# Moving three small steps of a Householder tridiagonalisation between VectorE and GpSimd, and dropping a negated scalar

## The chip, the cores and the metric

The kernel runs on one core of a Trainium2 chip. The metric is the device time of one execution in microseconds, as the median of several runs. Engines are called by their names in the profile: PE (TensorE, matrix products), PEld (TensorE loading weights), DVE (VectorE), ACT (ScalarE), POOL (GpSimd) and SP (SyncE, which issues the DMAs here).

## The reference

Two graph layers run one after the other over 64 items x of 256 x 256 (float32), with one shared 256 x 256 matrix `adj`. Cut to what matters:

```python
h = relu(layernorm(x))
# layer 0: G = adj * adj, three products with weights, G applied in each
y = relu(G @ (h @ W1)); y = relu(G @ (y @ W2)); x = x + G @ (y @ W3)

h = relu(layernorm(x))
# layer 1: eigenvectors of the normalized Laplacian of adj
deg = adj.sum(0) + adj.sum(1) - diag(adj); d = rsqrt(deg)
U = eigh(d[:, None] * (diag(deg) - adj) * d[None, :]).vectors
x = x + U @ (relu(U.T @ h @ L1_W1 + b1) @ L1_W2 + b2)
```

Layer 0 needs nothing of the eigenvectors. Layer 1 needs them, and layer 0's result.

## The kernel before, in words

**Two works side by side.** The eigenvectors U of a 256 x 256 symmetric matrix are found by one long chain of dependent steps: a reduction to tridiagonal form (`tridiagonalize`, lines 410 to 553), the eigenproblems of 16 small leaves (`leaves`), and a merge in four levels (`level`). That chain uses mostly VectorE with small operands. Meanwhile TensorE works off layer 0 for 32 pairs of items (`Layers.products`, with matmuls of 128x512 and 128x256), and ScalarE empties its PSUM banks. When the eigenvectors are there, layer 1 runs over the same 32 pairs (`layer1`).

**Who decides the order.** On TensorE and ScalarE the order is written down when the program is built, by `Pace` (lines 147 to 230). Pace keeps a clock for each engine and reckons how long each operation of the eigenvector chain takes, from its engine and width (`Op`, lines 83 to 117: for VectorE 0.065 us plus 0.06 for a scalar from memory plus an amount by width, for GpSimd 0.2 us plus an amount by width, all times 1.06 for the chain). Each time the chain wants an operation, Pace first issues layer-0 operations that start before the chain's operation is due. On the chip TensorE then runs that list strictly in order: if the chain is later than Pace reckoned, TensorE stands at the chain's transposes; if it is earlier, the chain waits for the layer-0 products ahead of it. Layer-0 work that finds no place beside the chain is issued beside the first pairs of layer 1 (`pace.finish()` in line 2070 issues what is left). On VectorE and GpSimd the order is chosen by a scheduler of the tile framework. All issued operations of the chain carry line 192 in the profile, so they are told apart by their tiles.

**One column of the reduction.** The loop in line 470 runs over 254 columns. Column `k` with `lo = k + 1` below 128 works on both halves of the 256 rows (`halves = [0, 1]`, 127 columns, called the wide half here); from 128 on only the second half is left (the narrow half). The matrix `a` lies in SBUF as two halves of 128 partitions x 256. `xr` holds the current column as a row on all partitions, `xc` the same as a column. In each column:

- `rs` and `qs` and from them `nb` (line 484) give the sign and length of the reflection. `nb` and `alpha` are columns of the tile `m1`, the sums of squares (`tail`) of `m2`; all three show as `m` in the profile.
- `xa` (line 482) is the product of the two halves of `a` with `xr`, one wide operation for each half, tile `r` in the profile; `ac` (line 487) adds the own column.
- TensorE turns `ac` and the matrix's own column into rows, `pu` (psB) and `pr` (psA), with transposes against the identity (line 488).
- Beside that, `u1` (line 496) is the first element of the reflection vector, written into `xr`; `den` (line 497) the divisor, `none` a guard against a zero column; `gam` (line 498) its reciprocal (tile `z`, column k); `uc` (line 499, tile `q`) the vector as a column; `ngam` (line 500) is `gam` with its sign turned; `gg` and `gu` are products with it.
- `gc` and `gr` (lines 504 and 508) are the products scaled with `ngam`; `uau` is their scalar product; `both`, `f` and `xn` (lines 511 to 513) make the next column as a row, `xcn` (lines 525 to 527) the same as a column, with a mask from `lower` in line 527.
- Four wide operations (lines 532 and 533, two for each half) update `a`, tile `A`.
- `below` and `length` (lines 443 to 462) start the next column's length: `alpha` on GpSimd, the sum of squares on ScalarE in the wide half, `q` and `qn` on the engine `aside(lo)`, which is GpSimd in the wide half and VectorE in the narrow half. `none` is on GpSimd in both.

GpSimd's queue in a column of the wide half is, in this order: `alpha` (a copy into m), `q`, `none`, `qn`, `none`, `qs`, `gg`, `gu`. It issues no DMA; all DMAs are issued by SP.

```python
aside = lambda lo: nc.gpsimd if lo < P else nc.vector
```

Of the kernel before, what the change touches and what calls it, by code (L numbers as in the profile page):

```python
# [23 lines left out]
OP = mybir.AluOpType  # L24
# [4 lines left out]
P = 128  # L29
# [222 lines left out]
class Eigen:  # L252
# [44 lines left out]
    def row(self, tag):  # L297
        return self.mp.tile([P, N], F32, tag=tag, name=tag)
# [111 lines left out]
    def tridiagonalize(self, a):  # L410

        nc = self.nc
        ident = self.ident
        us, gams = self.mat("q2"), self.row("z2")
        drow, erow = self.row("D"), self.row("E")  # L420
        nc.vector.memset(erow[:, N - 1 : N], 0.0)
        nc.vector.memset(us[:, :, N - 2 : N], 0.0)
        nc.vector.memset(gams[:, N - 2 : N], 0.0)

        def as_row(tag, column, halves):
            ps = self.psum(tag)
            for h in halves:
                nc.tensor.transpose(
                    ps[:, h * P : (h + 1) * P],
                    column[:, h : h + 1].to_broadcast([P, P]),  # L430
                    ident[:, 0, 0:P],
                )
            return ps

        row = lambda tag: self.sp.tile([P, N], F32, tag=tag, name=tag)
        guard = self.col("guard", 1)
        nc.vector.memset(guard, 1e-30)
        book = self.mat("m1")
        alphas, nbs, tails = book[:, 0, :], book[:, 1, :], self.mat("m2")[:, 0, :]

        aside = lambda lo: nc.gpsimd if lo < P else nc.vector

        def below(xr, lo):

            rest = slice(lo + 1, N)
            sq, tail, alpha = self.row("junk"), *(t[:, lo - 1 : lo] for t in (tails, alphas))
            if lo < P:
                nc.scalar.activation(sq[:, rest], xr[:, rest], AF.Square, accum_out=tail)
            else:
                self.stt(sq[:, rest], xr[:, rest], 1.0, xr[:, rest], OP.mult, OP.mult, accum=tail)  # L450
            nc.gpsimd.tensor_copy(alpha, xr[:, lo : lo + 1])
            return alpha, tail

        def length(xr, lo, tail):

            nn, s0, q, qn = (self.col(c, 1) for c in ("nn", "s0", "q", "qn"))
            x1 = xr[:, lo : lo + 1]
            self.stt(nn, x1, x1, tail, OP.mult, OP.add)
            nc.scalar.activation(s0, nn, AF.Sqrt, bias=guard)
            aside(lo).tensor_scalar(q, x1, 0.0, 0.5, OP.is_ge, OP.subtract)  # L460
            aside(lo).tensor_tensor(qn, q, nn, OP.mult)
            return nn, s0, q, qn

        xc = self.col("xc")
        self.tt(xc, a[:, :, 0], self.lower[:, :, 0], OP.mult)
        xr = row("xr")
        nc.vector.tensor_copy(xr, as_row("psB", xc, [0, 1])[:, 0:N])
        alpha, tail = below(xr, 1)
        nn, s0, q, qn = length(xr, 1, tail)
        for k in range(N - 2):  # L470
            lo = k + 1
            r, rest = slice(lo, N), slice(lo + 1, N)
            halves = [0, 1] if lo < P else [1]
            hs = slice(halves[0], H)
            rc = a[:, :, lo]

            rs, qs, nb = self.col("rs", 1), self.col("qs", 1), nbs[:, k : k + 1]
            self.recip(rs, s0)
            aside(lo).tensor_tensor(qs, q, s0, OP.mult)
            xa, junk = self.col("xa"), self.row("r0")  # L480
            for h in halves:
                self.stt(junk[:, r], a[:, h, r], 1.0, xr[:, r], OP.mult, OP.mult, accum=xa[:, h : h + 1])
                if h == halves[0]:
                    self.stt(nb, rs, qn, qs, OP.mult, OP.add)

            ac, uc = self.col("ac"), us[:, :, k]
            self.stt(ac[:, hs], rc[:, hs], nb, xa[:, hs], OP.mult, OP.add)
            pu, pr = as_row("psB", ac, halves), as_row("psA", rc, halves)

            none = self.col("none", 1)  # L490
            nc.gpsimd.tensor_scalar(none, tail, 1e-30, 1e30, OP.is_le, OP.mult)
            nc.gpsimd.tensor_tensor(none, none, nn, OP.add)
            den, ngam, gg, gu = (self.col(c, 1) for c in ("den", "ngam", "gg", "gu"))
            gam = gams[:, k : k + 1]
            u1 = xr[:, lo : lo + 1]
            self.ts(u1, u1, nb, OP.add)
            self.stt(den, alpha, nb, none, OP.mult, OP.add)
            self.recip(gam, den)
            self.stt(uc, ident[:, :, lo], nb, xc, OP.mult, OP.add)
            self.ts(ngam, gam, -1.0, OP.mult)  # L500
            aside(lo).tensor_tensor(gg, gam, gam, OP.mult)
            aside(lo).tensor_tensor(gu, gg, u1, OP.mult)
            gc, gr = self.col("gc"), row("gr")
            self.ts(gc[:, hs], ac[:, hs], ngam, OP.mult)

            uau, c = self.col("uau", 1), self.col("c", 1)
            self.stt(junk[:, r], pu[:, r], 1.0, xr[:, r], OP.mult, OP.mult, accum=uau)
            self.ts(gr[:, r], pu[:, r], ngam, OP.mult)

            xn, xcn, both, f = row("xr"), self.col("xc"), self.row("r1"), self.col("f", 1)  # L510
            self.stt(both[:, rest], gr[:, rest], u1, pr[:, rest], OP.mult, OP.add)
            self.stt(f, uau, gu, gr[:, lo : lo + 1], OP.mult, OP.add)
            self.stt(xn[:, rest], xr[:, rest], f, both[:, rest], OP.mult, OP.add)
            more = lo + 1 < N - 1
            if more:
                alpha1, tail1 = below(xn, lo + 1)
            self.stt(c, uau, 0.5, gg, OP.mult, OP.mult)
            wr, wc = row("wr"), self.col("wc")
            self.stt(wr[:, r], xr[:, r], c, gr[:, r], OP.mult, OP.add)
            self.stt(wc[:, hs], uc[:, hs], c, gc[:, hs], OP.mult, OP.add)  # L520
            if more and halves[0]:
                following = length(xn, lo + 1, tail1)
            if halves[0]:
                nc.gpsimd.memset(xcn[:, 0:1], 0.0)
            self.stt(xcn[:, hs], gc[:, hs], u1, rc[:, hs], OP.mult, OP.add)
            self.stt(xcn[:, hs], uc[:, hs], f, xcn[:, hs], OP.mult, OP.add)
            self.tt(xcn[:, hs], xcn[:, hs], self.lower[:, hs, lo], OP.mult)
            if more and not halves[0]:
                following = length(xn, lo + 1, tail1)

            for h in halves:
                self.stt(a[:, h, r], wr[:, r], uc[:, h : h + 1], a[:, h, r], OP.mult, OP.add)
                self.stt(a[:, h, r], xr[:, r], wc[:, h : h + 1], a[:, h, r], OP.mult, OP.add)
            xr, xc = xn, xcn
            if more:
                alpha, tail, (nn, s0, q, qn) = alpha1, tail1, following

        done = slice(0, N - 2)
        e0 = self.row("r1")[:, done]
        self.tt(e0, nbs[:, done], alphas[:, done], OP.add)  # L540
        self.ts(tails[:, done], tails[:, done], 1e-30, OP.is_gt)
        self.tt(e0, e0, tails[:, done], OP.mult)
        self.tt(erow[:, done], alphas[:, done], e0, OP.subtract)

        nc.vector.tensor_copy(erow[:, N - 2 : N - 1], xr[:, N - 1 : N])
        dc = self.col("dnew")
        junk = self.row("junk")
        for h in range(H):
            self.stt(junk, a[:, h, :], 1.0, ident[:, h, :], OP.mult, OP.mult, accum=dc[:, h : h + 1])
        pb = self.psum("psB")  # L550
        self.spread(pb[:, 0:N], dc, ident)
        self.ts(drow, pb[:, 0:N], 1.0, OP.add)
        return drow, erow, us, gams
# [1593 lines left out]
```

## Time and profile before

| | |
|---|---|
| median of 3 runs | 2461.46 us (2460.98 to 2461.79) |
| the profiled execution | 2461.43 us, its span in the profile 2459.6 us |
| PE busy over the span | 2397.0 us (97%), 8986 matmuls |
| PEld busy | 1545.5 us (63%) |
| DVE busy | 2147.1 us (87%), 13352 instructions |
| ACT busy | 1008.9 us (41%) |
| POOL busy | 475.5 us (19%), 1625 instructions |
| wide half of the reduction | 21.45 to 781.83 us |
| narrow half | 781.83 to 1332.40 us |
| leaves, levels, eigenvectors | to 2261.6 us |
| layer 1 | to the end |

Busy time is the time in which an engine has an instruction in work. VectorE's instructions overlap: the next one starts before the one ahead has written its last element, so what an instruction costs in a row of others is the distance of the starts. A matrix product of float32 stands as two matmuls in the trace. In lines of the timeline, the columns are start in us, duration in us, engine, line, operation, output<-inputs, shapes, count, and in brackets the idle time before it and what ended it. Buffer numbers are left out of names, so that `m` is any column of the tile m1 or m2, and `A` the matrix.

### The profile page before, as it was taken

How to read it: one execution, taken by the hardware profiler on the slowest of the kernel's cores; microseconds unless marked ns; L12 is line 12 of the kernel's file. 1: busy time of each engine (PE TensorE's matmuls, PEld its weight loads, DVE VectorE, ACT ScalarE, POOL GpSimd, SP SyncE). 2: the span in 40 equal slices, each digit the busy share in tenths (PEclk: the TensorE clock that was granted, in tenths of full speed). 3: DMA queues.
4: the chain of work that ended last, by engine and by line, in shares of the span. 5: the costliest groups of instructions: out<-in, count | busy, mean ns of one | idle time of the engine just before them, and what ended most of it. 6: DMA issues, size and time to landing. Idle time of an engine off the chain costs nothing. (4 is left out here: it accounts for less than half of the span.)

```text
span 2459.6 us, 38181 instructions
## 1 busy us (share of the span) xinstructions
PE 2397.0 (97%) x8986; PEld 1545.5 (63%) x8986; DVE 2147.1 (87%) x13352; ACT 1008.9 (41%) x2827; POOL 475.5 (19%) x1625
## 2 busy tenths in 40 slices
PE   7999999999999999999999999999999999999999
PEld 4666655666555566655556666655566666666888
DVE  7999999999999999999999989888887888885333
ACT  4334444434444433444444244443434344443322
POOL 2333333333333111111111000000000000000443
PEclk9999999999999999999999999999999999999999
DMA  3000000000000000000000000000000000001476
GB/s 112 18 5 23 22 18 23 22 22 6 22 21 20 22 23 14 14 23 22 18 23 30 10 22 22 22 22 18 22 22 27 20 8 22 22 22 36 167 256 202
DMA packets 59401, 90.02 MB, mean 37 GB/s; under 512 B 5793, under 2 KB 42785, under 8 KB 59169
## 3 DMA queue, kind: packets, MB, share of 16 engines
q1 hardware_dynamic: 59168, 87.52, 10.6%
q8 instruction: 73, 1.20, 0.2%
q14 instruction: 160, 1.30, 0.2%
HBM read 47.13 MB, written 40.37 MB: 36 GB/s over the span
## 5 line engine op out<-in xcount | busy, mean ns | idle before, releaser
L192 PE MATMUL bank<-y,L_gnn_W 128*128 128x512 f32 x2048 | 906.5, 593 | 0.3 <-ACT y L192 0.3
L192 PEld LDWEIGHTS bank<-y,L_gnn_W 128*128 128x128 f32 x2048 | 379.3, 190 | 427.6 <-issue 409.4
L192 PE MATMUL bank<-L_gnn_W,s 128*128 128x256 f32 x2048 | 464.6, 379 | 1.7 <-ACT s L192 1.6
L192 PEld LDWEIGHTS bank<-L_gnn_W,s 128*128 128x128 f32 x2048 | 382.1, 190 | 51.4 <-ACT s L192 2.0
L192 ACT ACTIVATE s<-bank 128x512 f32<-128x512 f32 x384 | 224.8, 587 | 188.3 <-PE bank L192 187.1
L192 PE MATMUL bank<-gt,s 128*128 128x256 f32 x1024 | 230.5, 379 | 2.0 <-ACT s L192 2.0
L192 PE MATMUL bank<-L_gnn_W,y 128*128 128x512 f32 x512 | 228.9, 593 | 0.0
L192 PEld LDWEIGHTS bank<-gt,s 128*128 128x128 f32 x1024 | 191.9, 190 | 37.0 <-issue 9.8
L192 ACT ACTIVATE s<-nn,guard 128x1 f32<-128x1 f32 x254 | 74.3, 293 | 244.9 <-DVE nn L192 230.5
L192 ACT ACTIVATE junk<-xr 128x254 f32<-128x254 f32 (+63 forms) x127 | 45.9, 361 | 285.1 <-DVE xr L192 276.9
L192 POOL COPY m<-xr 128x1 f32<-128x1 f32 x254 | 55.9, 220 | 545.8 <-DVE xr L192 537.2
L192 PEld LDWEIGHTS bank<-L_gnn_W,y 128*128 128x128 f32 x512 | 95.8, 191 | 99.0 <-issue 95.9
L192 ACT COPY y<-bank 128x512 f32<-128x512 f32 x192 | 110.9, 581 | 112.3 <-PE bank L192 111.2
L192 ACT ACTIVATE h<-x,shift,scale 128x256 f32<-128x256 f32 x256 | 135.7, 590 | 49.6 <-DVE shift L192 49.4
L192 ACT ACTIVATE junk<-x,nm 128x256 f32<-128x256 f32 x256 | 129.0, 504 | 27.6 <-DVE nm L192 23.2
L192 DVE SCALAR_TENSOR_TENSOR A<-xr,wc,A 128x255 f32<-128x255 f32 (+63 forms) x381 | 139.1, 367 | 0.0
L192 DVE SCALAR_TENSOR_TENSOR A<-wr,q,A 128x255 f32<-128x255 f32 (+63 forms) x381 | 138.2, 365 | 0.0
L192 DVE SCALAR_TENSOR_TENSOR q<-q 128x1 f32<-128x1 f32 (+1 forms) x576 | 119.5, 208 | 20.1 <-ACT q L192 9.8
L192 ACT ACTIVATE junk<-x 128x256 f32<-128x256 f32 x256 | 105.4, 412 | 74.9 <-DVE x L192 65.1
L192 PEld LDWEIGHTS psB<-ident,ac 128*128 128x128 f32 x381 | 44.9, 135 | 144.2 <-PE bank L192 77.8
L192 PE MATMUL bank<-gt,h 128*128 128x256 f32 x512 | 120.6, 386 | 3.8 <-DVE den L192 3.8
L192 POOL TENSOR_TENSOR xb<-x,ub 128x512 f32<-128x512 f32 x16 | 19.8, 1275 | 511.3 <-DMA hw<-hw 489.5
(615 smaller groups left out, 4421.5 us busy)
## 6 DMA issues: line engine op xcount, KB each, us to landing
x<-x SPq DMA_DIRECT2D x60, 512.0 KB, 3.6
x<-in_x_dram SPq DMA_DIRECT2D x64, 256.0 KB, 3.7
out_dram<-out SPq DMA_DIRECT2D x64, 256.0 KB, 2.2
hw<-hw SPq DMA_DIRECT2D x60, 256.0 KB, 2.6
L_gnn_W<-in_L_gnn_W_dram SPq DMA_DIRECT2D x1, 2048.0 KB, 10.8
L_gnn_W<-in_L_gnn_W_dram SPq DMA_DIRECT2D x1, 1024.0 KB, 13.3
L_gnn_W<-in_L_gnn_W_dram SPq DMA_DIRECT2D x1, 512.0 KB, 6.2
mask<-in_c_blk_dram SPq DMA_DIRECT2D x2, 256.0 KB, 2.6
```

Of the source, the lines that this page charges most:

```text
L192: return op.call(*op.args, **op.kwargs)
```

## The change

`ngam` is gone: `gc` and `gr` are scaled with `gam` itself and so have the other sign, and the operations that use them subtract instead of adding. In the wide half `den` becomes two operations on GpSimd (a product and a sum) in place of one on VectorE, `u1` is added on GpSimd, and the mask of the next column (line 527) goes to `aside(lo)`, which is GpSimd there. In the narrow half `den`, `u1` and the mask stay on VectorE. The planner's reckoning follows the new operations by itself, so the order on TensorE and ScalarE changes too.

```diff
-            den, ngam, gg, gu = (self.col(c, 1) for c in ("den", "ngam", "gg", "gu"))
+            den, gg, gu = (self.col(c, 1) for c in ("den", "gg", "gu"))
             gam = gams[:, k : k + 1]
             u1 = xr[:, lo : lo + 1]
-            self.ts(u1, u1, nb, OP.add)
-            self.stt(den, alpha, nb, none, OP.mult, OP.add)
+            if lo < P:
+                nc.gpsimd.tensor_tensor(den, alpha, nb, OP.mult)
+                nc.gpsimd.tensor_tensor(den, den, none, OP.add)
+                nc.gpsimd.tensor_tensor(u1, u1, nb, OP.add)
+            else:
+                self.ts(u1, u1, nb, OP.add)
+                self.stt(den, alpha, nb, none, OP.mult, OP.add)
             self.recip(gam, den)
             self.stt(uc, ident[:, :, lo], nb, xc, OP.mult, OP.add)
-            self.ts(ngam, gam, -1.0, OP.mult)
             aside(lo).tensor_tensor(gg, gam, gam, OP.mult)
             aside(lo).tensor_tensor(gu, gg, u1, OP.mult)
...
-            self.ts(gc[:, hs], ac[:, hs], ngam, OP.mult)
+            self.ts(gc[:, hs], ac[:, hs], gam, OP.mult)
...
-            self.ts(gr[:, r], pu[:, r], ngam, OP.mult)
+            self.ts(gr[:, r], pu[:, r], gam, OP.mult)
...
-            self.stt(both[:, rest], gr[:, rest], u1, pr[:, rest], OP.mult, OP.add)
-            self.stt(f, uau, gu, gr[:, lo : lo + 1], OP.mult, OP.add)
-            self.stt(xn[:, rest], xr[:, rest], f, both[:, rest], OP.mult, OP.add)
+            self.stt(both[:, rest], gr[:, rest], u1, pr[:, rest], OP.mult, OP.subtract)
+            self.stt(f, uau, gu, gr[:, lo : lo + 1], OP.mult, OP.subtract)
+            self.stt(xn[:, rest], xr[:, rest], f, both[:, rest], OP.mult, OP.subtract)
...
-            self.tt(xcn[:, hs], xcn[:, hs], self.lower[:, hs, lo], OP.mult)
+            aside(lo).tensor_tensor(xcn[:, hs], xcn[:, hs], self.lower[:, hs, lo], OP.mult)
```

The lines left out are those of `wr`, `wc` and `xcn`, with `OP.subtract` in place of the last `OP.add` in each.

More of the change, by code (lines that the diff above doesn't have):

```diff
@@ L518, in tridiagonalize @@
             wr, wc = row("wr"), self.col("wc")
-            self.stt(wr[:, r], xr[:, r], c, gr[:, r], OP.mult, OP.add)
-            self.stt(wc[:, hs], uc[:, hs], c, gc[:, hs], OP.mult, OP.add)
+            self.stt(wr[:, r], xr[:, r], c, gr[:, r], OP.mult, OP.subtract)
+            self.stt(wc[:, hs], uc[:, hs], c, gc[:, hs], OP.mult, OP.subtract)
             if more and halves[0]:
@@ L524, in tridiagonalize @@
                 nc.gpsimd.memset(xcn[:, 0:1], 0.0)
-            self.stt(xcn[:, hs], gc[:, hs], u1, rc[:, hs], OP.mult, OP.add)
-            self.stt(xcn[:, hs], uc[:, hs], f, xcn[:, hs], OP.mult, OP.add)
-            self.tt(xcn[:, hs], xcn[:, hs], self.lower[:, hs, lo], OP.mult)
+            self.stt(xcn[:, hs], gc[:, hs], u1, rc[:, hs], OP.mult, OP.subtract)
+            self.stt(xcn[:, hs], uc[:, hs], f, xcn[:, hs], OP.mult, OP.subtract)
+            aside(lo).tensor_tensor(xcn[:, hs], xcn[:, hs], self.lower[:, hs, lo], OP.mult)
             if more and not halves[0]:
```

## The prediction

> **What bounds the kernel now.** I read the stages first: each engine's busy time in the wide half of the tridiagonal form (127 columns, 21.45 to 781.83 us) and the narrow half (to 1332.40). Columns: stretch, length, PE, PEld, DVE, ACT, POOL busy.
>
> ```profile
> 21.45:781.83 760.38, 744.53 (x2811) 464.16 (x2810) 730.71 (x3975) 342.18 (x1049) 287.54 (x1013) 1.00 0.06 19
> 781.83:1332.40 550.57, 538.39 (x2005) 333.38 (x2003) 535.01 (x4276) 225.08 (x612) 98.68 (x503) 1.00 0.06 18
> ```
>
> TensorE and VectorE are both about 97% busy, so I asked what TensorE waits for there (engine, what it was to do, releaser: total, times, longest), and looked at one column on it.
>
> ```profile
> PE psB L192 <- DVE xr L192: 23.7, 66, 0.8
> ```
>
> ```profile
> 300.96 0.38 PE L192 MATMUL psB<-ident,ac 128*128 128x128 f32 x2
> ...
> 301.39 4.91 PE L192 MATMUL bank<-L_gnn_W,s 128*128 128x256 f32 x22
> 306.93 0.40 PE L192 MATMUL psB<-ident,ac 128*128 128x128 f32 x2 [0.62 <-DVE xr L192]
> ```
>
> TensorE runs in order. Between two columns' transposes it does the layer-0 products that Pace put there when the program was written. The starts of matmuls follow each other by 0.109 us (128 wide), 0.216 (256) and 0.429 (512); so this column holds 4 x 0.109 + 22 x 0.216 = 5.19 us of work, but its period is 306.93 - 300.96 = 5.97, and 0.78 is lost to the VectorE chain. The other columns' periods read the same way: a column takes the longer of its planned TensorE work and its chain. Over the wide half the work is 727 us of 760 (33 lost), over 126 periods of the narrow half 527 of 549 (22 lost). All layer-0 and layer-1 products have to run somewhere, and after the eigenvectors TensorE goes on without gaps. So **the time is TensorE's fixed work plus what it loses**; a shorter chain gains only as losses shrink.
>
> Now the chain, VectorE from m (nb in the code) to the first read of psB:
>
> ```profile
> 299.99 0.22 DVE L192 SCALAR_TENSOR_TENSOR m<-rs,qn,qs 128x1 f32<-128x1 f32 x1
> 300.12 0.37 DVE L192 SCALAR_TENSOR_TENSOR r<-A,xr 128x212 f32<-128x212 f32 x1
> ...
> 300.42 0.21 DVE L192 SCALAR_TENSOR_TENSOR den<-m,none 128x1 f32<-128x1 f32 x1
> 300.55 0.21 DVE L192 SCALAR_TENSOR_TENSOR ac<-A,m,xa 128x2 f32<-128x2 f32 x1
> 300.68 0.21 DVE L192 TENSOR_SCALAR xr<-xr,m 128x1 f32<-128x1 f32 x1
> 300.81 0.15 DVE L192 RECIPROCAL z<-den 128x1 f32<-128x1 f32 x1
> 300.88 0.20 DVE L192 SCALAR_TENSOR_TENSOR q<-ident,m,xc 128x2 f32<-128x2 f32 x1
> 301.00 0.15 DVE L192 TENSOR_SCALAR ngam<-z 128x1 f32<-128x1 f32 x1
> 301.18 0.23 DVE L192 TENSOR_SCALAR gc<-ac,ngam 128x2 f32<-128x2 f32 x1
> 301.45 0.22 DVE L192 SCALAR_TENSOR_TENSOR xc<-gc,xr,A 128x2 f32<-128x2 f32 x1
> 301.58 0.37 DVE L192 SCALAR_TENSOR_TENSOR r<-psB,xr 128x212 f32<-128x212 f32 x1
> ```
>
> That is 1.59 us. And GpSimd beside VectorE at the end of the same column:
>
> ```profile
> 303.88 0.43 DVE L192 SCALAR_TENSOR_TENSOR A<-wr,q,A 128x212 f32<-128x212 f32 x1
> 303.90 0.49 POOL L192 TENSOR_SCALAR q<-xr 128x1 f32<-128x1 f32 x1
> ...
> 304.47 0.47 POOL L192 TENSOR_SCALAR none<-m 128x1 f32<-128x1 f32 x1
> ...
> 305.21 0.39 POOL L192 TENSOR_TENSOR none<-none,nn 128x1 f32<-128x1 f32 x1
> ...
> 305.49 0.43 DVE L192 SCALAR_TENSOR_TENSOR A<-xr,wc,A 128x212 f32<-128x212 f32 x1
> 305.56 0.41 POOL L192 TENSOR_TENSOR qs<-q,s 128x1 f32<-128x1 f32 x1
> 306.01 0.22 DVE L192 SCALAR_TENSOR_TENSOR m<-rs,qn,qs 128x1 f32<-128x1 f32 x1
> ```
>
> GpSimd's one-element operations take 0.19 alone (gg, gu) but 0.39 to 0.49 here, and each ends 0.05 to 0.09 after a wide VectorE operation; m starts 0.04 after qs. VectorE follows A by 0.35 when nothing holds it, so m (0.52 after A) already waits 0.17 for GpSimd.
>
> **The Trainium skill.** "SBUF — State Buffer", section "Who interferes with whom": a VectorE instruction with two SBUF inputs and a GpSimd instruction that reads SBUF exclude each other; whichever issues second waits for the whole of the first. The trace agrees on GpSimd's side: q, none and qs end with the A updates. No VectorE instruction is stretched in it.
>
> **The change, part by part.** The emitted order of the new program, which holds no times, gives what moves.
>
> *Planned work.* Pace reckons with the new operations and puts less layer-0 work under each column. By the starts above the wide half gets 698 us instead of 727 (-29), the narrow half 521.5 instead of 526.8 (-5). These 34 us return later; that moves nothing in the total. What counts is whether the chain shrinks as much: 0.23 us a column in the wide half.
>
> *den, u1 and the column mask to GpSimd (wide half).* Its queue becomes alpha, q, mask, none, qn, none, qs, den, den, u1, gg, gu: 12 instead of 8, all in order, no DMA among them. (a) The mask stands ahead of qs. It takes the slot beside one wide VectorE operation, so each later one moves on a slot, and qs finds none left: it runs alone after the last A. VectorE itself is 0.07 earlier (the mask's slot there). That A ends at 305.85; qs is issued 0.04 before and takes 0.19, done about 306.04, m 306.08 instead of 306.01: **+0.07**. (b) From m on: m ends at 0.22, den's product can start 0.08 later (z end to gg start: 300.96 to 301.04) but is held by r<-A,xr until 0.50, done 0.55; the sum 0.08 later (gg end to gu start), 0.19 long, done 0.82; the reciprocal at 0.85. gc follows 0.19 later as ngam did (1.04), xc 0.27 (1.31), r<-psB 0.13 (1.44 instead of 1.59): **-0.15**. The transposes don't bind: ac to r<-psB needs 0.80 at the shortest, and 0.56 + 0.80 = 1.36. u1 follows den and is done near 1.0, before xc asks. So -0.08 in 96 columns. (c) In 31 columns, nearly all among the first 60, the scheduler put the reciprocal and uc *ahead of ac*. There the wait for den holds ac and with it TensorE: reciprocal 0.85, uc 0.92, ac 1.04, r<-psB 1.84: +0.25, with (a) **+0.32**. Bounds: at best qs costs nothing and den is not held (done 0.76, reciprocal 0.80): 1.36 to 1.39 against 1.59, about -0.23, and +0.20 where ac is behind. At worst (a) costs a whole GpSimd turn more (+0.2), and den's steps or ac exclude each other once: +0.20 and +0.55. I take the middle: 31 x 0.32 - 96 x 0.08 = +2 us of chain.
>
> *ngam.* In the wide half its slots are in (b). In the narrow half nothing goes to GpSimd; z to gc was ngam's own dependent step and falls from 0.38 to 0.26: -0.12 a column, -15 us of chain against -5 of work. The sign flips are the same instructions with subtract: nothing.
>
> *Sum.* For every column I took the longer of planned work and chain, the chain read from columns in which TensorE waits (6.56 us less 0.012 per column in the wide half, 0.50 more where a layer-0 addition lies in it and 0.067 for each of its small steps), letting a column absorb 0.24 us of TensorE's lateness, 0.12 after the change and none in (c). For before this gives 33 and 22 lost, as measured. After: 62 in the wide half (mean chain 5.96, mean work 5.50: 127 x 0.46 = 58, and 4 where work is longer) and 16 in the narrow. (62 - 33) + (16 - 22) = **+22 us** (+0.9%). The profiled execution took 2461.43, with 1.8 around its span of 2459.6, and the median is 2461.46, so 2461.4 + 22 = **2484 us**. If the plan's loss in the later stages (25 us of TensorE gaps in leaves and levels) falls differently, some 6 us either way.
>
> **Rivals.** *A, faster.* GpSimd delivers den before VectorE asks for the reciprocal, which then costs no wait. VectorE's removed slots (u1 0.13, den 0.13, ngam's step 0.12, mask 0.07: 0.45 a column) come off the chain, twice what the plan gave up: the sum gives -22, 2439. It decides from 0.19 a column on. For: VectorE is 96% busy. Against: r<-A,xr lies just where den must read, and m already waits for qs.
> *B, no net change:* the best ends of (a) to (c) give +7 (2468), and with smaller gaps later, 2462.
> *C, the exclusion bites harder:* +0.20 and +0.55 a column give +54, 2515; then wide VectorE rows would be stretched, which the trace of before doesn't show with 8 operations.
> That the parts don't move as said is excluded by the emitted order.
>
> **Numbers.** Forecast case (2470 to 2500) 0.62; A 0.10; B 0.12; C 0.16. Under about 0.2% (5 us) a measurement of this kernel can't be told from no change: faster 0.09, same 0.12, slower 0.79. The range runs from 2460, which leaves A and little else below, to 2512, the upper end of the bounds.
>
> **What would show it.** TensorE's wait for psB rises from 24 us to over 50; the wide half still takes about 760 us with fewer matmuls in it; GpSimd's qs ends alone, after the last A; the reciprocal waits for den about 0.3; in the first 60 columns ac comes 0.5 later after m. The narrow half is 10 us or more shorter. It is wrong if the wide half shrinks by over 24 us (A), or if VectorE's wide rows lengthen (C).

## The result and the profile after

The changed kernel takes **2487.31 us** (median of 4 runs, 2486.16 to 2488.75); the kernel before took 2461.22 beside it (4 runs). The ratio is 1.0107, 95% interval 1.0094 to 1.0121: slower by 26 us. The profiled execution has a span of 2486.5 us.

The stages of the changed kernel, in the columns of before (stretch, length, PE, PEld, DVE, ACT, POOL busy): the wide half, then the narrow half.

```profile
22.38:784.18 761.80, 719.90 (x2727) 446.69 (x2726) 704.88 (x3454) 327.58 (x1007) 366.85 (x1517) 1.00 0.05 17
784.18:1323.41 539.23, 530.74 (x1935) 322.29 (x1935) 523.73 (x4165) 231.01 (x638) 97.61 (x504) 1.00 0.06 20
```

The reader is to compare length and number of matmuls. The wide half is as long as before (761.8 against 760.4 us) with 84 matmuls fewer in it; GpSimd is 79 us busier, VectorE 26 us less busy. The narrow half is 11.3 us shorter.

I call *work* what the distances of the matmuls' starts make of a stage (0.109, 0.216 and 0.429 us, as in the prediction), and *loss* its length less its work. What TensorE waited for in both halves, changed kernel (engine, what it was to do, releaser: total, times, longest); lines of at most 1.2 us are left out:

```profile
PE psB L192 <- DVE ac L192: 32.3, 65, 1.2
PE psB L192 <- DVE xr L192: 7.4, 16, 1.1
PE psB L192 <- DVE q L192: 4.9, 8, 1.5
PE psB L192 <- DVE z L192: 1.7, 2, 1.5
```

The waits for the transposes into psB grew from 23.7 us (the line of before in the prediction; the others there are at most 0.6) to 46.3 in these four lines, and the longest from 0.8 to 1.5. The view names only the part of the loss that stands as a wait.

A column of the changed kernel in which `ac` goes ahead of the reciprocal, 96 of the 127 are like it (start, duration, engine, line, operation, output<-inputs):

```profile
302.97 0.22 DVE L192 SCALAR_TENSOR_TENSOR nn<-xr,m 128x1 f32<-128x1 f32 x1
303.04 0.22 POOL L192 TENSOR_TENSOR xc<-xc,lower 128x2 f32<-128x2 f32 x1
303.11 0.43 DVE L192 SCALAR_TENSOR_TENSOR A<-xr,wc,A 128x213 f32<-128x213 f32 x1
303.34 0.29 POOL L192 TENSOR_SCALAR none<-m 128x1 f32<-128x1 f32 x1
...
304.17 0.43 DVE L192 SCALAR_TENSOR_TENSOR A<-xr,wc,A 128x213 f32<-128x213 f32 x1
304.25 0.41 POOL L192 TENSOR_TENSOR qs<-q,s 128x1 f32<-128x1 f32 x1
304.69 0.22 DVE L192 SCALAR_TENSOR_TENSOR m<-rs,qn,qs 128x1 f32<-128x1 f32 x1
304.82 0.37 DVE L192 SCALAR_TENSOR_TENSOR r<-A,xr 128x212 f32<-128x212 f32 x1
304.99 0.26 POOL L192 TENSOR_TENSOR den<-m 128x1 f32<-128x1 f32 x1 [0.33 <-DVE m L192]
...
305.32 0.20 POOL L192 TENSOR_TENSOR den<-den,none 128x1 f32<-128x1 f32 x1
305.48 0.18 POOL L192 TENSOR_TENSOR xr<-xr,m 128x1 f32<-128x1 f32 x1
305.56 0.17 DVE L192 RECIPROCAL z<-den 128x1 f32<-128x1 f32 x1
305.62 0.40 PE L192 MATMUL psB<-ident,ac 128*128 128x128 f32 x2 [0.62 <-DVE ac L192]
305.76 0.26 DVE L192 TENSOR_SCALAR gc<-ac,z 128x2 f32<-128x2 f32 x1
306.12 0.22 DVE L192 SCALAR_TENSOR_TENSOR xc<-gc,xr,A 128x2 f32<-128x2 f32 x1
306.26 0.37 DVE L192 SCALAR_TENSOR_TENSOR r<-psB,xr 128x212 f32<-128x212 f32 x1
```

From the start of m: den's product done at 0.56, the sum at 0.83, the reciprocal at 0.87, gc at 1.07, `xcn` at 1.43, the first read of psB at 1.57. Before it stood at 1.59. TensorE has worked off what was planned for this column and stands 0.62 until `ac` is there.

And one of the 31 columns with the reciprocal ahead of `ac`:

```profile
88.93 0.22 DVE L192 SCALAR_TENSOR_TENSOR m<-rs,qn,qs 128x1 f32<-128x1 f32 x1
89.07 0.41 DVE L192 SCALAR_TENSOR_TENSOR r<-A,xr 128x245 f32<-128x245 f32 x1
89.23 0.29 POOL L192 TENSOR_TENSOR den<-m 128x1 f32<-128x1 f32 x1 [0.33 <-DVE m L192]
89.60 0.19 POOL L192 TENSOR_TENSOR den<-den,none 128x1 f32<-128x1 f32 x1
89.82 0.16 DVE L192 RECIPROCAL z<-den 128x1 f32<-128x1 f32 x1 [0.34 <-POOL den L192]
89.90 0.20 DVE L192 SCALAR_TENSOR_TENSOR q<-ident,m,xc 128x2 f32<-128x2 f32 x1
90.02 0.21 DVE L192 SCALAR_TENSOR_TENSOR ac<-A,m,xa 128x2 f32<-128x2 f32 x1
90.38 0.40 PE L192 MATMUL psB<-ident,ac 128*128 128x128 f32 x2 [0.43 <-DVE ac L192]
90.82 0.41 DVE L192 SCALAR_TENSOR_TENSOR r<-psB,xr 128x245 f32<-128x245 f32 x1
```

VectorE stands 0.34 for `den`, `ac` starts 1.09 after m, TensorE waits 0.43 for it, and psB is read at 1.89. Over the wide half that wait of VectorE is:

```profile
DVE z L192 <- POOL den L192: 10.0, 34, 0.3
```

### The profile page after: what moved, and what is told of

The parts are those of the page before. It is cut to its first block, busy times and chain, and to the rows that moved or that the text cites. A ratio compares the mean times of both kernels' runs of the same rounds, so it can differ in the third digit from the quotient of the medians.

```text
span 2486.5 us, 38157 instructions
## 1 busy us (share of the span) xinstructions
PE 2399.9 (97%) x8986; PEld 1545.1 (62%) x8986; DVE 2106.9 (85%) x12717; ACT 1007.1 (41%) x2827; POOL 554.1 (22%) x2133
## 5 line engine op out<-in xcount | busy, mean ns | idle before, releaser
L192 ACT ACTIVATE junk<-x,nm 128x256 f32<-128x256 f32 x256 | 129.1, 504 | 30.1 <-DVE nm L192 25.6
L192 PE MATMUL psB<-ident,ac 128*128 128x128 f32 x381 | 87.0, 283 | 50.4 <-DVE ac L192 32.3
```

The costliest lines, as they stand in the source:

```text
L192: return op.call(*op.args, **op.kwargs)
```

## The experiments

My theory was that of the forecast: Pace plans less layer-0 work under each column, the chain gets hardly shorter, and TensorE loses the difference. Against it stood that the loss comes only from the 31 columns with `ac` late; that VectorE and GpSimd stretch each other's wide operations (rival C); and that one of the moved steps does all the harm. The stages of every kernel's profiled execution, all in us:

| kernel | median | ratio to before, 95% interval | wide: length, work, loss | narrow: length, work, loss | leaves and levels: loss |
|---|---|---|---|---|---|
| before | 2461.4 | | 760.4, 727.2, 33.2 | 550.6, 526.8, 23.8 | 24.4 |
| changed | 2487.3 | 1.0107 (1.0094 to 1.0121) | 761.8, 697.9, 63.9 | 539.2, 521.5, 17.7 | 25.6 |
| e1 sign only | 2449.6 | 0.9953 (0.9936 to 0.9969) | 745.4, 718.6, 26.8 | 539.0, 518.1, 20.9 | 21.2 |
| e2 mask only | 2469.9 | 1.0033 (1.0020 to 1.0046) | 756.2, 711.7, 44.5 | 549.8, 525.0, 24.8 | 22.5 |
| e3 den and u1 only | 2485.5 | 1.0097 (1.0081 to 1.0114) | 772.9, 712.6, 60.3 | 549.2, 524.1, 25.1 | 21.2 |
| e4 `ac` first | 2480.0 | 1.0076 (1.0059 to 1.0093) | 755.1, 697.9, 57.2 | 539.3, 521.5, 17.8 | 25.7 |
| e5 u1 back | 2466.2 | 1.0023 (1.0015 to 1.0032) | 754.1, 704.8, 49.3 | 540.6, 521.9, 18.7 | 17.3 |
| e6 changed, more planned | 2453.6 | 0.9972 (0.9962 to 0.9982) | 766.2, 733.2, 33.0 | 538.3, 517.3, 21.0 | 19.0 |
| e7 before, more planned | 2451.0 | 0.9960 (0.9946 to 0.9974) | 768.5, 747.4, 21.1 | 547.0, 522.9, 24.1 | 23.0 |
| e8 sign, more planned | 2437.3 | 0.9908 (0.9891 to 0.9924) | 760.6, 746.1, 14.6 | 539.0, 518.2, 20.9 | 22.3 |
| e9 sign, early memset | 2447.8 | 0.9946 (0.9930 to 0.9963) | 745.2, 718.6, 26.6 | 538.6, 518.1, 20.4 | 21.3 |
| e10 changed, mended | 2444.9 | 0.9937 (0.9920 to 0.9953) | 757.4, 733.2, 24.2 | 538.4, 517.3, 21.1 | 19.0 |
| e11 sign, more planned in all | 2434.4 | 0.9893 (0.9876 to 0.9909) | 760.0, 746.1, 14.0 | 547.6, 531.9, 15.7 | 24.6 |
| e12 sign, second wait | 2451.4 | 0.9964 (0.9952 to 0.9977) | 748.6, 718.6, 30.0 | 538.2, 518.1, 20.1 | 21.1 |

TensorE's work over the whole program is 2354 us in each of them; what a stage doesn't hold stands in a later one. Leaves and levels run to the last transposes into psA. Each ratio is to the kernel before as measured in the same round, where its median lay between 2460.0 and 2461.4.

### The three parts, one at a time

**e1, the sign alone.** The branch on `lo < P` and the move of the mask are taken out of the changed kernel:

```diff
-            if lo < P:
-                nc.gpsimd.tensor_tensor(den, alpha, nb, OP.mult)
-                nc.gpsimd.tensor_tensor(den, den, none, OP.add)
-                nc.gpsimd.tensor_tensor(u1, u1, nb, OP.add)
-            else:
-                self.ts(u1, u1, nb, OP.add)
-                self.stt(den, alpha, nb, none, OP.mult, OP.add)
+            self.ts(u1, u1, nb, OP.add)
+            self.stt(den, alpha, nb, none, OP.mult, OP.add)
...
-            aside(lo).tensor_tensor(xcn[:, hs], xcn[:, hs], self.lower[:, hs, lo], OP.mult)
+            self.tt(xcn[:, hs], xcn[:, hs], self.lower[:, hs, lo], OP.mult)
```

> Only the sign change in both halves; den, u1 and mask stay on VectorE. Planned TensorE work by the emitted order: wide half 718.6 us (before 727.2, changed kernel 697.9), narrow half 518.1 (526.8, 521.5). Theory P (TensorE loses the planned work that the chain does not give back): ngam's step comes off the chain, 0.12 us a column in both halves, against 8.6 us of planned work in each half, so losses of about 27 (wide) and 19 (narrow), together 9 us less than before: 2452. Rival O (the order of reciprocal and ac in 31 columns makes the whole loss): no such column here, so no more than the sign's gain, 2446 to 2452. If the chain of the wide half does not shrink without ngam (the wait moves to TensorE's rows), 2465.

Measured 2449.6, **11.8 us faster** than before. The wide half's stage line:

```profile
22.69:768.07 745.38, 733.24 (x2792) 460.56 (x2790) 717.06 (x3836) 338.40 (x1030) 287.91 (x1012) 1.00 0.06 19
```

Its work fell by 8.6 us, its length by 15.0: the dropped step `ngam` was on the chain, and it comes off by more than the plan gave up. m to the first read of psB is 1.47 (median; 1.61 before). The narrow half shrank by 11.6, all that the change reaches there.

**e2, the mask alone**, in the kernel before:

```diff
-            self.tt(xcn[:, hs], xcn[:, hs], self.lower[:, hs, lo], OP.mult)
+            aside(lo).tensor_tensor(xcn[:, hs], xcn[:, hs], self.lower[:, hs, lo], OP.mult)
```

> Only the mask of the next column goes to GpSimd in the wide half; ngam, den and u1 as before. Planned work 711.7 us in the wide half (-15.4). Theory P: the slot gives the chain nothing, since nn behind it waits for ScalarE's sum of squares in any case, so the loss rises by the planned work: +14 to +17 us, 2475 to 2478. Rival Q (the mask ahead of qs in GpSimd's queue makes m late by 0.07): +25 us, 2486. If VectorE's slot counts (0.07 off each column): +8 us, 2469.

Measured 2469.9, 8.5 us slower, less than I held likely and equal to the last case, in which VectorE's slot counts. Work fell by 15.5 us, the length by 4.2, which is 0.03 a column and not 0.07. VectorE gains little of the mask's place, as a look at what follows it shows. First the kernel before, then e2 (`nn` is the first step of `length` for the next column):

```profile
304.07 0.19 ACT L192 ACTIVATION_READ_ACCUMULATOR junk<-xr 128x1 f32 x1
304.23 0.15 DVE L192 TENSOR_TENSOR xc<-xc,lower 128x2 f32<-128x2 f32 x1
304.30 0.21 DVE L192 SCALAR_TENSOR_TENSOR nn<-xr,m 128x1 f32<-128x1 f32 x1
```

```profile
307.88 0.19 ACT L192 ACTIVATION_READ_ACCUMULATOR junk<-xr 128x1 f32 x1
308.10 0.22 DVE L192 SCALAR_TENSOR_TENSOR nn<-xr,m 128x1 f32<-128x1 f32 x1
```

In both, `nn` starts 0.03 to 0.04 after ScalarE's sum of squares is there (304.26 and 308.07). The mask lay in a place where VectorE had to wait anyway; from the A ahead to nn it is 0.40 before and 0.38 in e2 (medians over the wide half; in the two columns shown the difference is lost). So the mask is worth 0.02 to 0.03 to the chain, and 0.12 to the plan (15.5 us over 127 columns).

**e3, den and u1 alone**, in the kernel before:

```diff
-            self.ts(u1, u1, nb, OP.add)
-            self.stt(den, alpha, nb, none, OP.mult, OP.add)
+            if lo < P:
+                nc.gpsimd.tensor_tensor(den, alpha, nb, OP.mult)
+                nc.gpsimd.tensor_tensor(den, den, none, OP.add)
+                nc.gpsimd.tensor_tensor(u1, u1, nb, OP.add)
+            else:
+                self.ts(u1, u1, nb, OP.add)
+                self.stt(den, alpha, nb, none, OP.mult, OP.add)
```

> Only den and u1 go to GpSimd in the wide half; ngam and mask as before. Planned work 712.6 us in the wide half (-14.6), 35 columns with the reciprocal ahead of ac. Theory P with the wait for den: chain +0.32 in those 35 columns and unchanged in the others gives +27 us, 2488. Rival: GpSimd's work comes for nothing and the two VectorE slots (0.26) come off the chain: below 2450. Rival E (GpSimd's reads hold up VectorE's wide rows): above 2495, with r<-A,xr longer than 0.37.

Measured 2485.5, 24 us slower: alone almost as much as the whole change. The wide half gets *longer* (772.9) with 14.6 us less work in it. The time came near what was expected, but by another split: column for column, m to the read of psB grew by 0.27 in the 35 columns (0.32 expected) and by 0.13 in the 92 others, where nothing was expected (medians). There gc to `xcn` alone grew by 0.07; what that is, e5 and e12 ask. The three parts sum to -11.8 + 8.5 + 24.1 = +21 us, the change to +26; the intervals of the single ratios are some 3 us to either side, so the difference isn't read.

### Where the chain loses it

**e4, `ac` held ahead of the reciprocal**, in the changed kernel:

```diff
-            self.stt(ac[:, hs], rc[:, hs], nb, xa[:, hs], OP.mult, OP.add)
+            made = self.stt(ac[:, hs], rc[:, hs], nb, xa[:, hs], OP.mult, OP.add)
...
-            self.recip(gam, den)
+            with self.tc.issue_after(made.ins):
+                self.recip(gam, den)
```

> The changed kernel with the reciprocal queued behind ac on VectorE in every column; planned TensorE work is the same as in the changed kernel (697.9 and 521.5). Theory P with the order as a part: the 31 columns give back about 0.3 us each, 9 us: 2478 (loss of the wide half about 57 instead of 64). Rival O (the order is the whole cause): the loss falls back to before's, 2455 to 2461. If the order costs nothing: 2487.

Measured 2480.0, 7.3 us less than the changed kernel, in the wide half alone (761.8 to 755.1), and there in the 31 columns alone: their periods, m to m, shrank by 6.9 us together (0.22 each), the others grew by 0.2 together. m to psB is now 1.57 over all columns (median). So the late `ac` is real, and it is 7 of the 26 us. That it is the whole cause is refuted.

**e5, u1 back on VectorE**, in the changed kernel:

```diff
-                nc.gpsimd.tensor_tensor(u1, u1, nb, OP.add)
+                self.ts(u1, u1, nb, OP.add)
```

> The changed kernel with u1 on VectorE again; den and mask stay on GpSimd. Planned TensorE work 704.8 us in the wide half (changed kernel 697.9), 521.9 in the narrow half; 30 columns with the reciprocal ahead of ac. Theory W (xc is slow because it now waits for GpSimd's u1 beside VectorE's gc): gc to xc falls from 0.363 to about 0.295, as with the sign change alone; with 7 us more planned work that gives 2479 to 2482. Rival (gc to xc is slow because gg or gu hold VectorE up): stays 0.36 and the time is 2480 to 2487 by the planned work alone.

Measured 2466.2, 21 us less, far below what I expected. The forecast had u1 at no cost, since it "is done near 1.0, before xc asks". In e5, gc to `xcn`:

```profile
303.93 0.26 DVE L192 TENSOR_SCALAR gc<-ac,z 128x2 f32<-128x2 f32 x1
304.22 0.22 DVE L192 SCALAR_TENSOR_TENSOR xc<-gc,xr,A 128x2 f32<-128x2 f32 x1
```

0.29, against 0.36 in the changed kernel (305.76 to 306.12), though u1 was there at 305.66, long before `xcn` asked. The difference is that `xcn` there has two engines to wait for: VectorE for gc, GpSimd for u1. In the profiled executions the loss of the wide half is 14.6 us lower: it is 7.7 us shorter and holds 6.9 us more work, since u1 counts on VectorE again. 8.3 us more are gaps in leaves and levels, where the chain is the same program and only the pieces that Pace has left over differ; why they fit better there wasn't tested. So the wide half accounts for some 13 of the 21 us, and the other 8 lie outside it.

**e9 and e12, the second wait by itself.** In e1's kernel, a memset on GpSimd of one column of `xcn`, which the next operation overwrites, makes `xcn` wait for GpSimd as well. In e9 it was put beside the tile's allocation:

```diff
+            if lo < P:
+                nc.gpsimd.memset(xcn[:, 0:1], 0.0)
```

> The sign change alone, with a memset of the first element of xcn added on GpSimd ahead of xc's first step in the wide half (the step writes over it). It reads nothing and is done long before, so it adds nothing but a second engine that xc has to wait for. Planned TensorE work is the same (718.6 and 518.1). Theory W (a VectorE instruction that waits for two engines starts about 0.07 later): gc to xc goes from 0.295 to 0.36, 127 x 0.07 = 8.6 us more chain, 2455 to 2458. Rival (in the changed kernel xc was held by gg and gu reading beside it): gc to xc stays 0.295, 2449 to 2450.

Measured 2447.8, gc to xc 0.294. The scheduler issued the memset a column early, and no second wait was left when `xcn` came: the run tells nothing of the question, only that the extra operation on GpSimd itself costs nothing that these times show. In e12 it is held behind qs:

```diff
-            aside(lo).tensor_tensor(qs, q, s0, OP.mult)
+            made = aside(lo).tensor_tensor(qs, q, s0, OP.mult)
+            if lo < P:
+                with self.tc.issue_after(made.ins):
+                    nc.gpsimd.memset(xcn[:, 0:1], 0.0)
```

> The sign change alone with the same memset of xcn's first element on GpSimd, now queued right behind qs, so that it lies in the same column ahead of xc and xc really waits for both engines (in the run before, the scheduler had put it a column early and no second wait was left). The memset reads nothing and is done some 0.8 us before xc asks. Planned TensorE work as with the sign change alone (718.6 and 518.1). Theory W: gc to xc 0.295 becomes 0.36 and the time 2454 to 2458. Rival (xc is held by gg and gu, not by its second wait): 0.295 and 2448 to 2450.

A column of e1, then of e12:

```profile
303.26 0.26 DVE L192 TENSOR_SCALAR gc<-ac,z 128x2 f32<-128x2 f32 x1
303.56 0.22 DVE L192 SCALAR_TENSOR_TENSOR xc<-gc,xr,A 128x2 f32<-128x2 f32 x1
```

```profile
300.92 0.26 DVE L192 TENSOR_SCALAR gc<-ac,z 128x2 f32<-128x2 f32 x1
301.29 0.22 DVE L192 SCALAR_TENSOR_TENSOR xc<-gc,xr,A 128x2 f32<-128x2 f32 x1
```

The medians over the wide half are 0.295 and 0.364: **0.07 for a second engine to wait for**, though it has long been done (the memset 1.4 us before `xcn`, median). The trace also shows what it goes with. Between gc and `xcn` of the changed kernel VectorE's queue holds one instruction more, which does nothing but wait (duration in ns, least, median and most; first and last start):

```profile
L192 DVEq EVENT_SEMAPHORE  x1: 21/21/21, 306.1 to 306.1; - x1
```

It starts 0.04 after gc's end, and `xcn` 0.07 after it. In the changed kernel 119 of the 127 columns have it, with gc to `xcn` at 0.363 (median). Eight do not: in six of them `xcn` follows gc by 0.29 as in e1, though u1 comes from GpSimd there too, and in the other two something else holds it. Before, e1, e5 and e9 have it in no column, e12 in 110.

The time, 2451.4, is below what the theory gave and lies between those of the two cases, so it decides nothing; the wide half's length and loss rose by 3.2 us. 127 x 0.07 would be 9. But in 66 columns, in e1 or in e12, the read of psB starts over 0.16 after `xcn`, since it waits for TensorE's transposes, and there m to the read didn't change (0.00, median); in the other 61 it grew by 0.06, 3.7 us together.

### Is it the plan?

**e6, e7, e8: the same kernels with 1.10 in place of 1.06** as Pace's factor for the chain in the wide half. Nothing that the engines compute or wait for is edited; Pace puts more layer-0 work under each column (in e6 the scheduler puts the reciprocal ahead of `ac` in 28 columns, not 31). The line goes into the changed kernel (e6), into that of before (e7) and into e1's (e8):

```diff
             lo = k + 1
+            self.pace.slower = 1.10 if lo < P else self.pace.SLOWER
```

> The changed kernel, but Pace reckons the chain of the wide half 1.10 instead of 1.06 times as long, so that planned TensorE work there is 733.2 us (before 727.2, changed kernel 697.9), 517.3 in the narrow half. Nothing on the chain is touched. Theory P: the chain of the wide half stays at some 762 us and TensorE's loss in it falls from 64 to about 33 us, narrow 18: 2456 to 2462. Rival C (the new chain itself is longer and costs the time, whatever is planned): the wide half gets longer by the added 35 us, 2487.

> The kernel before with the same 1.10 in the wide half: planned work 747.4 us (727.2 at 1.06), narrow 522.9. Theory P: the wide half takes about 768 us instead of 760, its loss falls from 33 to 21, narrow 25: 2452. If the kernel before was balanced and the chain is pushed back as much as TensorE gains: 2461.

> The sign change alone with the same 1.10 in the wide half: planned work 746.1 us (718.6 at 1.06), narrow 518.2. Theory P: chain 745 us with 718.6 planned; now both are about equal, wide half about 757, loss 11 to 15 instead of 27, narrow 20: 2434 to 2439, the fastest so far. If layer 0 runs out before the eigenvectors are there, TensorE stands in the last level and the gain is lost: 2449.

The wide half of e6, then e8:

```profile
22.10:788.28 766.18, 749.98 (x2826) 465.89 (x2824) 708.61 (x3470) 345.81 (x1060) 365.24 (x1517) 1.00 0.06 18
```

```profile
20.74:781.38 760.64, 754.61 (x2872) 478.39 (x2870) 722.23 (x3850) 351.07 (x1066) 287.89 (x1012) 1.00 0.06 19
```

e6: 2453.6, **33 us less than the changed kernel by the plan alone** (each against before in its own round). The wide half is 4.4 us longer and holds 35.2 us more work; a chain that costs the time whatever is planned (this run's rival C) would have made it some 35 us longer. So the place of the loss is shown: TensorE had too little to do under a column that took as long as before. The plan was short for every version, though: in the same way e7 gains 9.5 us over before and e8 11 over e1. At the same factor the change stands at +2.6 us against before (2453.6 and 2451.0), which the intervals, 2 to 3 us to either side, hardly tell from nothing, and the sign alone at -13.7.

**e10, the moves at their best:** the changed kernel with e4's order, e5's u1 and e6's line.

```diff
+            self.pace.slower = 1.10 if lo < P else self.pace.SLOWER
...
-                nc.gpsimd.tensor_tensor(u1, u1, nb, OP.add)
+                self.ts(u1, u1, nb, OP.add)
...
+            with self.tc.issue_after(made.ins):
+                self.recip(gam, den)
```

> The change with its three faults taken out: u1 on VectorE, the reciprocal behind ac in every column, and Pace's 1.10 in the wide half (planned 733.2 us, narrow 517.3). Only den, its product and sum, and the mask stay on GpSimd. Theory P: chain about 0.08 a column under the kernel before (m to r<-psB 1.50 instead of 1.59), wide half about 750 us, loss 17 to 20, narrow 19: 2443 to 2448, slower than the sign change alone with the same 1.10 (2437). If moving den pays once its faults are gone: below 2437.

2444.9. Faster than before, and still 7.6 us behind e8, the sign alone under the same factor. Its wide half is 3.2 us shorter than e8's but has 12.9 us less work in it: again the plan gives up more than the chain. Whether a factor above 1.10 would close that wasn't run.

**e11, e8 with more planned in the narrow half and the leaves too:**

```diff
-    SLOWER, IN_BLOCKS = 1.06, 1.13
+    SLOWER, IN_BLOCKS = 1.06, 1.10
...
-            self.pace.slower = 1.10 if lo < P else self.pace.SLOWER
+            self.pace.slower = 1.10 if lo < P else 1.09
```

> The sign change alone with Pace's 1.10 in the wide half, 1.09 in the narrow half and 1.10 instead of 1.13 in the leaves, which takes back what the narrow half now holds: planned 746.1 and 531.9 us (narrow before 526.8), about 9 us of layer 0 left at the end of the eigenvectors as with 1.10 in the wide half alone. Theory P: narrow loss 21 falls to 13, the wide half as it was, the leaves no worse: 2429 to 2433. If the leaves wait more with less work planned beside them: 2437.

2434.4, 26 us faster than before in its round (ratio 0.9893, 0.9876 to 0.9909) and the fastest of all, though just over what I expected: the narrow half still loses 15.7, and leaves and levels 24.6.

## Why the prediction was right, step by step

**The sum.** (62 - 33) + (16 - 22) was forecast; the stages give (63.9 - 33.2) + (17.7 - 23.8) = +24.6, and 1.2 in leaves and levels, together +25.8 for the measured 26. As printed the forecast's terms make 23, not 22; and the narrow half before lost 23.8 by its stage line (550.6 less 526.8), not 22. Neither moves the result much. The planned work (-29 and -5) came as said, since it is in the program. That "a column takes the longer of its planned TensorE work and its chain" is what e6 shows.

**(a), the mask ahead of qs: wrong.** +0.07 was forecast because "qs finds none left: it runs alone after the last A". In the column above qs runs beside the last A as before (304.25 to 304.66; A ends at 304.60), and m follows 0.03 later. From the start of the last A to m it is 0.51 in both kernels (median). The step that failed is the mask's "slot": it didn't take one beside a wide operation but ran beside the short `nn` (303.04 to 303.26, 0.07 ahead of the next A). `none` behind it then ends 0.09 after the same A as before, only its wait is shorter (0.27 long instead of 0.44, medians), so no later operation moves on. The -0.07 for the mask's place on VectorE failed too: it was 0.02 to 0.03, since `nn` waits for ScalarE (e2). So +0.07 was forecast for (a), the mask's gain already taken off, and -0.02 came.

**(b), from m to the read of psB: mechanism right, one term wrong.** Product 0.55, sum 0.82, reciprocal 0.85 were forecast; 0.56, 0.83, 0.87 came, and u1 was done at 0.97 (near 1.0). The Trainium skill's rule, "SBUF — State Buffer", section "Who interferes with whom", that an operation that issues second waits for the first, priced den rightly: it ended 0.06 after r<-A,xr. The term that failed is "xc 0.27 (1.31)": it was 0.36. 0.07 of it is the second engine (e5, e12); 0.03 is gc itself, which takes 0.26 where gg starts just behind it (e1 has it too) and 0.23 before and in the 31 columns, where gg starts ahead of it; what lengthens it wasn't tested. So the forecast's -0.15 became -0.02 in this column (1.59 to 1.57) and -0.03 over the 96 (median of each column less the same column before). That u1 costs nothing because it is done before `xcn` asks was wrong: its being on another engine cost the 0.07.

**(c), 31 columns with `ac` late: right.** 1.04 and 1.84 after m were forecast for `ac` and the read of psB, 1.08 and 1.89 came (medians), 0.26 over the same columns before (0.25 forecast); e4 gives back 0.22 for each of them.

**Net chain.** 31 x 0.32 - 96 x 0.08 = +2 us was forecast. With the medians, and 0.02 for the mask, it is 31 x (0.26 - 0.02) - 96 x (0.03 + 0.02) = +3 us. (a) was too dear by 0.09 in 127 columns, 11 us, and (b) too cheap by 0.12 in 96, 12 us. That these two cancel is luck, and so is the small change in leaves and levels, which moved by 8 us between the changed kernel and e5. What was foreseen is the frame: in the wide half the plan gives up 29 us and the chain nearly nothing.

**ngam: right.** The narrow half is 11.3 us shorter (10 or more was forecast); z to gc fell there from 0.38 to 0.27 (0.26 was forecast), and from 0.38 to 0.20 in the wide half.

**The signs.** TensorE's waits for psB rose to 46, not over 50. VectorE stands 0.3 for den in 34 columns, as forecast; elsewhere that view shows no such wait. That qs ends alone, after the last A, didn't come. The rivals: A needed 0.19 a column off the chain and got 0.05 in 96 columns, and 0.24 more chain in 31; C needed stretched wide rows, and r<-A,xr at 212 columns takes 0.37 before and after, and none of the 504 updates of A compared with the same one before is longer by more than 0.03.

## What to carry to other kernels

When a planner puts one engine's work under another's chain, price a step that moves by two numbers: what it takes off the chain, and what the planner takes out of its plan for it. With the planner's reckoning left as it is, only where the first is the larger does the move gain; in the wide half ngam's step was such a one (15.0 us of length for 8.6 of work), the mask was not (4.2 for 15.5), and den and u1 even lengthened it (by 12.5, with 14.6 less work). Then ask whether the plan itself is short: one factor in it gained 33 us here in the changed kernel and 9.5 in the kernel before. Before a step is taken off a busy engine, look at what its successor waits for: the mask lay in a place where that engine had to wait anyway. And look at how many engines the successor will wait for afterwards.

## What the runs showed of the hardware that was not expected

- `xcn`, a VectorE instruction, starts 0.07 us later when it waits for VectorE and GpSimd than when it waits for VectorE alone, even if GpSimd is long done (0.295 and 0.364 in e1 and e12; 0.296 and 0.363 in e5 and the changed kernel). In the trace one of the two waits is then an instruction of its own in VectorE's queue, in 119 of the changed kernel's 127 columns; six columns without it don't have the 0.07.
- A GpSimd operation that is held up beside a VectorE operation of two tensors ended just behind that one, also where the next VectorE operation was under way by then: the mask 0.06 after `nn` (median), with A started 0.07 after the mask; `none` 0.09 after its A, in both kernels. VectorE's wide operations weren't lengthened by it in any run: every A and r<-A,xr is within 0.04 of the same one in the kernel before. The Trainium skill ("Perfetto Trace Analysis", section "Optimizing Scalar/DVE Operations") says that moving work between VectorE and GpSimd may not help since they share a port. At the factors that were run it didn't help here (e10 7.6 us behind e8), but no run shows the port as the cause on VectorE's side; what the runs show is the second wait, den ending 0.06 behind the wide row, and the plan.
